# A four-layer transformer on one core: the first batch of relative attention sent through DRAM before the tables, and the experts' gate weights spread one group ahead with the last group closed in halves

## The chip, the cores and the metric

The kernel runs on one core of a Trainium2 chip. The core has five engines with an instruction queue each: TensorE (PE, matrix products into PSUM; its weight loads are shown as PEld), VectorE (DVE), ScalarE (ACT), GpSimd (POOL) and SyncE (SP, which here issues every DMA). The metric is the device time of one execution in microseconds, as the median of the runs. All data is float32.

## The reference, cut to what matters

Four layers, each followed by a residual sum and a layer norm over the last axis (128):

```
x = norm(x + relative_attention(x))     # 16 batches of 256 tokens, 16 heads of 8
x = norm(x + local_layers(x))           # 6 rounds of windowed attention and feed-forward
x = norm(x + causal_attention(x))       # 16 heads of 8
x = norm(x + experts(x))                # 8 experts, the best 2 by gate
```

The change touches the first and the last. Relative attention adds to the plain logits three terms that depend on the clipped distance of the two positions:

```
a_q, a_k, a_v = Eq[rel], Ek[rel], Ev[rel]          # rel: distance clipped to -64..64
logits = (q.k + q.a_k + k.a_q + a_q.a_k) * scale
out = softmax(logits) @ v  +  sum over m of softmax(logits)[l, m] * a_v[l, m]
```

The experts compute, for every token, all eight experts and keep two:

```
gates = softmax(x @ gate_w);  the two best: sel (0 or 1), tok_w = sum of the two gates
h = gelu(x @ w1[e] + b1[e]);  y[e] = h @ w2[e] + b2[e]
out = sum over e of y[e] * sel[e] * tok_w
```

## The kernel before, in words

**Relative attention** (`relative_attention`) works on one batch of 256 tokens at a time, in eight turns per batch (`NU = 8`, the table `TURNS`). `run(at)` emits the steps of turn `at % 8`; a step marked -1 works for the next batch, 0 for this one, 1 for the last. The turns from -8 to -1 hold batch 0's preparation alone. In order these are: `turn` (L317, the tokens transposed on PE), `project` (L326, q and k; L336 adds an end term on POOL), `rearranged` for k and then for q, `diagonal` (L405, a mask multiplied in on POOL), `rq_half` and `rq_corners` from k, `rk_half` and `rk_corners` from q (L419 and L444 on PE, with ACT copying the rq results out at L458 and L467 and DVE adding the position table `pp` or `ppc` at L478 and L488). Turn 0 begins with batch 0's second `rk_half` and ends in the first `weights` (L513 and L525 on PE, L535 on DVE), which the exponentials (L551) and everything else of the batch follow.

`rearranged` is a round trip through DRAM: POOL permutes (L385, one buffer `r_perm` for k and q), four DMAs write the rows to DRAM (L388, `r_rowsk` or `r_rowsq`), and four more read them back spread over the partitions (L393, `r_dk` or `r_dq`), each after its rows have landed.

Ahead of these turns stand the tables. Two of them (`toeplitz`, L793 on PE, `tq` and `tk`) are built from the small tables `Eq` and `Ek`, which are loaded turned, one element at a time (L770); their end values (`eqb`, `ekb`) go into L336 and L346. `prod` and `frow` (L818 to L822) make a row that is written to DRAM (L824) and read back in sliding windows (`windows`, L840: `r_winp`, `r_winpc`; `r_winv` and `r_winvc` come from a table of `Ev` rows that L827 to L829 put into DRAM). PE turns the windows over with the matrix `anti` (L878), and DVE copies the results to `pp`, `ppc`, `tv`, `tvc` (L882, L884). Memsets clear the term tiles `r_rq` on POOL and `r_rkc` on DVE.

The order of the instructions within each of PE, ACT, DVE and POOL is that of the program from `first` on, set by `env.in_order(first)`, where `first` stands behind the tables; for the tables themselves, and for SP, a scheduler chooses it.

**Experts** (`experts`) takes the 16 batches in eight groups of two (512 tokens, four tiles of 128). `turn(g)` transposes the tokens (L1780), `score(h)` makes the gate values of half of the groups (L1793 on PE, maximum and difference on DVE, exponential on ACT at L1805), and `choose(h)` finds the two best by counting on DVE (L1812 to L1829, one step of it, L1821, on POOL) and writes them spread into `e_wide`. For each group, `first` multiplies by w1 (L1840) with the gelu on ACT (L1847), `turn_gates` transposes the gates (L1854, copied out by ACT at L1856 as `e_wT`), `weigh` spreads them over the experts' rows on PE (L1865) and multiplies them into the gelus on DVE (L1867, `e_hT`), `second` multiplies by w2 (L1876) and adds b2 (L1883), sums with the tokens on DVE (L1886), and takes the statistics (L1894, L1895 on DVE; L1897 to L1901 on POOL). `finish` scales on ACT (L1907) and stores (L1915). `small()` gives one of four PSUM banks, `big()` one of two pairs of banks, which `weigh` takes both. The order of the loop is

```
for g in range(NG):
    turn_gates(g + 1); first(g + NH); second(g); weigh(g + 1); finish(g - 1)
finish(NG - 1)
```

with the four first groups' `first`, `turn_gates(0)`, `weigh(0)` and `choose(1)` ahead of it; it is kept on PE, ACT, DVE and POOL by `env.in_order(begin)`.

## Time and profile before

| | |
|---|---|
| runs shown, us | 4129.33, 4126.4, 4128.36; median 4128.36 |
| profiled execution, us | 4126.21 |
| its span, us | 4124.3 |
| mean granted clock of PE | 0.991 |
| PE busy | 4012.5 us, 97% |
| first weights matmul of relative attention | at 57.45 us |
| first transposes of the experts | at 3997.94 us |
| last matmul of the experts | ends at 4115.0 us |

The page gives busy time by engine and by slices of the span; the chain of waits follows back from the last instruction what released each step. A timeline line has the start, the duration, the engine, the line of the kernel, what is written from what, and in brackets how long the engine stood idle before it and what ended that. Durations of matmul groups count from the first start to the last end. The granted clock is 1.00 at full speed.

### The profile page before, as it was taken

The page shows a single profiled execution, that of the slowest core. Times are in us where ns is not written, and L with a number is a line of the kernel's source. Part 1 is how long each engine was busy: PE and PEld are TensorE (multiplying, and loading weights), DVE is VectorE, ACT ScalarE, POOL GpSimd, SP SyncE. Part 2 cuts the span into 40 slices and gives each one's busy share as a digit, 9 for nine tenths or more (in the row PEclk, how much of TensorE's full clock was granted, in tenths as well). Part 3 has the DMA queues.
Part 4 walks back from the last instruction along what each step waited for, and adds up shares of the span by engine and source line. Part 5 has one row for each costly group of instructions (what it writes and reads, how often), then busy time and mean ns, then how long its engine had stood idle before and what let it go on. Part 6 is the DMA issues. An engine that isn't in the chain of part 4 may idle for free.

```text
span 4124.3 us, 141653 instructions
## 1 busy us (share of the span) xinstructions
PE 4012.5 (97%) x57932; PEld 2937.4 (71%) x57932; DVE 3285.5 (80%) x6379; ACT 3305.0 (80%) x11434; POOL 2783.4 (67%) x3334
## 2 busy tenths in 40 slices
PE   7999999899999999999999999999999999999998
PEld 5888888567677677667767776776777767656665
DVE  4666666788888888888888888888888888779974
ACT  3777766688888888888888888888888888879973
POOL 3333332788888888888888888888888888722221
PEclk8999999999999999999999999999999999999999
DMA  2101012100000000000000000000000000000000
GB/s 62 40 29 38 31 36 64 26 16 19 21 24 19 15 20 20 25 21 20 20 25 16 19 19 20 25 21 14 21 15 24 15 16 14 9 3 2 2 8 21
DMA packets 181813, 90.03 MB, mean 22 GB/s; under 512 B 142493, under 2 KB 173220, under 8 KB 181164
## 3 DMA queue, kind: packets, MB, share of 16 engines
q1 hardware_dynamic: 181164, 80.97, 7.4%
q8 instruction: 457, 7.49, 0.8%
q14 instruction: 192, 1.57, 0.1%
HBM read 38.49 MB, written 6.31 MB: 11 GB/s over the span
## 4 chain that ended last, share of the span: by engine, by line
PE 86%; POOL 6%; ACT 3%; issue 2%; DVE 1%; DMA 1%; SPq 0%; POOLq 0%; DVEq 0%; ACTq 0%
PE small L1250 16%; PE big L1100 12%; PE small L1157 8%; PE big L1225 7%; PE big L1172 5%; PE small L1347 3%; PE small L1331 3%; PE small L1315 3%; PE small L570 3%; PE big L525 3%; POOL a_u L1139 3%; PE small L1592 3%; PE big L1548 3%; PE big L513 3%; PE small L1225 2%
## 5 line engine op out<-in xcount | busy, mean ns | idle before, releaser
L1193 ACT ACTIVATE a_pr<-a_pr,a_nb 128x64 f32<-128x64 f32 x3072 | 1024.0, 338 | 5.7 <-DVE a_nb L1186 5.7
L1121 POOL TENSOR_TENSOR a_u<-a_u,a_r 128x1024 f32<-128x1024 f32 x384 | 901.3, 2371 | 25.9 <-DVE a_r L1116 21.2
L1139 POOL TENSOR_TENSOR a_u<-a_u,a_y 128x1024 f32<-128x1024 f32 x384 | 722.9, 1904 | 15.0
L1250 PE MATMUL small<-a_vo,a_g 128*128 128x128 f32 x6144 | 718.1, 275 | 1.6 <-DVE c_st L1465 1.6
L1250 PEld LDWEIGHTS small<-a_vo,a_g 128*128 128x128 f32 x6144 | 701.6, 192 | 2.6 <-ACT a_g L1243 2.5
L1111 ACT ACTIVATE a_sq<-big 128x1024 f32<-128x1024 f32 x384 | 391.4, 1021 | 260.2 <-PE big L1100 259.5
L1193 ACT ACTIVATION_READ_ACCUMULATOR a_pr<-a_pr,a_nb 128x1 f32 x3072 | 587.9, 191 | 0.0
L1157 PEld LDWEIGHTS small<-ident,a_u 128*128 128x128 f32 x3072 | 349.7, 141 | 142.8 <-POOL a_u L1139 91.0
L1128 DVE TENSOR_REDUCE a_ss<-a_sq 128x16 f32<-128x1024 f32 x384 | 445.6, 1200 | 0.0
L1157 PE MATMUL small<-ident,a_u 128*128 128x128 f32 x3072 | 402.3, 274 | 25.3 <-POOL a_u L1139 23.4
L1100 PE MATMUL big<-w_k,a_xs 128*128 128x512 f32 x768 | 382.0, 620 | 5.1 <-DVE a_r L1116 2.1
L1205 POOL TENSOR_TENSOR a_pr<-a_pr,a_rd 128x1024 f32<-128x1024 f32 x192 | 366.1, 1907 | 13.0 <-DVE a_rd L1204 13.0
L1100 PE MATMUL big<-w_q,a_xs 128*128 128x512 f32 x768 | 361.4, 593 | 0.0
L1172 PEld LDWEIGHTS big<-a_kT,a_qT 64*32 64x32 f32 x24576 | 261.4, 105 | 124.7 <-issue 74.8
L1180 DVE TENSOR_TENSOR a_pr<-big,w_band 128x1024 f32<-128x1024 f32 x192 | 234.6, 1222 | 109.0 <-PE big L1172 109.0
L535 DVE CUSTOM_DVE_ANT_0 r_lg<-big,r_rq 128x256 f32<-128x256 f32 x512 | 186.7, 421 | 152.7 <-PE big L525 126.4
L1112 DVE TENSOR_TENSOR a_u<-big,a_tak 128x1024 f32<-128x1024 f32 x192 | 235.1, 1224 | 83.9 <-ACT a_sq L1111 83.9
L1172 PE MATMUL big<-a_kT,a_qT 64*32 64x64 f32 x24576 | 293.1, 225 | 6.4 <-POOL a_kT L1150 3.5
L1233 ACT COPY a_g<-big 128x1024 f32<-128x1024 f32 x192 | 193.7, 1009 | 107.3 <-PE small L1225 106.8
L1100 PEld LDWEIGHTS big<-w_q,a_xs 128*128 128x128 f32 x768 | 142.6, 190 | 162.6 <-issue 127.4
L551 ACT ACTIVATE r_lg<-r_lg,r_nb 128x256 f32<-128x256 f32 x512 | 254.4, 508 | 2.8 <-DVE r_nb L535 2.8
L1574 ACT ACTIVATE c_lg<-c_lg,c_nb 128x256 f32<-128x256 f32 x512 | 255.6, 513 | 0.1
(290 smaller groups left out, 9316.9 us busy)
## 6 DMA issues: line engine op xcount, KB each, us to landing
a_xm<-a_xt SPq DMA_DIRECT2D x96, 96.0 KB
r_dk<-r_rowsk SPq DMA_DIRECT2D x64, 128.0 KB
r_dq<-r_rowsq SPq DMA_DIRECT2D x64, 128.0 KB
f_xt<-xa SPq DMA_DIRECT2D x96, 64.0 KB
f_xt<-xa SPq DMA_DIRECT2D x96, 63.5 KB
a_xt<-xa SPq DMA_DIRECT2D x80, 64.0 KB
a_xt<-xa SPq DMA_DIRECT2D x80, 63.5 KB
w_k<-in_L_ffn_Wqkv_dram SPq DMA_DIRECT2D x6, 512.0 KB
```

The lines of the kernel that those rows point to most:

```text
L1100: T.matmul(ps[:, c * 512 : (c + 1) * 512], lhsT=xs_of[i, b][:, t, 0:P], rhs=weights[i]["qk"[j]][:, c * 512 : (c + 1) * 512], start=True, s ...
L1111: A.activation(sq, ps3, AF.Square)
L1121: G.tensor_add(u, u, r)
L1128: V.tensor_reduce(ss[:, j], st[m]["sq", j], AX.X, ALU.add)
L1139: G.tensor_mul(u, u, bcast(y[:, j].unsqueeze(2), (P, H, DH)))
L1157: T.transpose(ps[:, k, :], u[:, o : o + P], ident)
L1172: T.matmul(ps[q0 : q0 + WIN, e, c, :], lhsT=qT[DH * e : DH * (e + 1), c, q0 : q0 + WIN], rhs=kT[DH * e : DH * (e + 1), c, t * P + q0 : t * ...
L1193: A.activation(s_["pr"][:, h], s_["pr"][:, h], AF.Exp, bias=s_["nb"][:, h : h + 1], accum_out=s_["den"][:, h : h + 1],)
L1205: G.tensor_mul(s_["pr"], s_["pr"], bcast(rd.unsqueeze(2), (P, H, DH)))
L1225: T.matmul(ps[win], lhsT=x[r, t, :], rhs=pT[r, :, o, :], start=(o == 0), stop=(o == 1),)
L1250: T.matmul(ps[:, 0:D], lhsT=st[m]["g"][:, h, :], rhs=weights[i]["vo"][:, h // 2, h % 2, :], start=(h == 0), stop=(h == H - 1),)
L1574: A.activation(lg[:, j], lg[:, j], AF.Exp, bias=nb[:, j : j + 1], scale=-1.0, accum_out=st[b, lc]["den"][:, h : h + 1],)
```

## The change

In relative attention the setup is reordered, and it is now in the program's order on SP too. Loads: x of batch 0, Wq, Wk, then Eq and Ek, the mask, `sel`, the `Ev` rows in DRAM, `anti`. Then batch 0 is turned and projected at once, and k is permuted and sent to DRAM (`there`); `rearranged` is split into `there` and `back`, and the sum with `eqb` is split off `project` as `shift` for batch 0. `prod` and `frow` come before the toeplitz tables. SP's order then is: k's rows, `r_winv`, k back, q's rows, `fx`, `r_winvc`, q back, `fe`, `r_winp`, `r_winpc`, and only then `ee`, `evs`, Wv, x of batch 1, `pick` and the other x. The memsets move behind the projection, those of `r_rq` clear only the half that is not written later, and the turned tables `pp`, `ppc`, `tvc` stand behind batch 0's first `rq_corners`.

In the experts `choose(h)` follows `score(h)` at once, `first` runs two groups ahead of the loop and three inside it, `weigh(g + 1)` stands before `second(g)` and `turn_gates(g + 2)` behind it. The last group is summed, normalised (on DVE) and stored in two halves, the first as soon as its half of `second` is done (`close`). Copies of the transposed tokens go to DVE for groups 1 and 3 alone, and four buffers hold the gelus instead of five.

```diff
-    def in_order(first):
+    def in_order(first, engines=ENGINES):
...
+            st[b].update(q=q, k=k)
+            if b:
+                shift(b)
+
+        def shift(b):
+            q, qe = st[b]["q"], fea.tile([P, S], F32, name="r_qe")
             for t in range(NT):
                 L = slice(t * P, (t + 1) * P)
                 G.tensor_scalar(qe[:, L], q[:, L], eqb[:, t : t + 1], None, ALU.add)
...
         def rearranged(b, n):
+            there(b, n)
+            back(b, n)
...
+            turn(0)
+            project(0)
+            there(0, "k")
...
+            winv = windows("v", evx, HD, P * HD, whole)
+            back(0, "k")
+            there(0, "q")
+            nc.sync.dma_start(fx, frow)
+            winvc = windows("vc", evx, HD, MAXD * HD, corner)
+            back(0, "q")
...
+            winp = windows("p", fx, 1, P, whole)
+            winpc = windows("pc", fx, 1, MAXD, corner)
...
+            nc.sync.dma_start(w["v"], I["L0_attn_Wv"])
+            load_x(1)
+            nc.sync.dma_start(pick, I["pick"].rearrange("p (g m) -> p g m", g=4))
+            shift(0)
+            for k in range(2):
+                G.memset(rq3[k][:, :, 1], 0.0)
+            turned(tv.rearrange("p s d -> p (s d)"), winv, HD, P * HD, None)
+            for k in range(2):
+                V.memset(rkc3[k], 0.0)
+            for at in range(-NU, -NU + 6):
+                run(at)
+            turned(pp, winp, 1, P, None)
+            turned(ppc, winpc, 1, MAXD, fe)
+            turned(tvc.rearrange("p s d -> p (s d)"), winvc, HD, MAXD * HD, ee)
...
+            if at == -NU + 6:
+                G.memset(spread, 0.0)
+            if at == -1:
+                G.memset(rq3[2][:, :, 1], 0.0)
+                V.memset(rkc3[2], 0.0)
...
-        env.in_order(first)
+        env.in_order(first, (*ENGINES, mybir.EngineType.SP))
...
+                if g == NG - 1 and k % NT == NT - 1:
+                    close(g, k // NT)
...
+        def close(g, j):
+            y = two.tile([P, NT, D], F32, name="e_yh")
+            added(y, g, j)
+            mv, rs = moments(y)
+            for t in range(NT):
+                V.tensor_scalar(
+                    y[:, t], y[:, t], mv[:, t, 0:1], rs[:, t : t + 1], ALU.subtract, ALU.mult
+                )
+            store(g, j, y)
...
             score(h)
-        choose(0)
-        for g in range(NH):
-            first(g)
+            choose(h)
+        first(0)
+        first(1)
         turn_gates(0)
         weigh(0)
-        choose(1)
+        first(2)
+        turn_gates(1)
         for g in range(NG):
-            if g + 1 < NG:
-                turn_gates(g + 1)
-            if g + NH < NG:
-                first(g + NH)
-            second(g)
+            if g + 3 < NG:
+                first(g + 3)
             if g + 1 < NG:
                 weigh(g + 1)
+            second(g)
+            if g + 2 < NG:
+                turn_gates(g + 2)
             if g:
                 finish(g - 1)
-        finish(NG - 1)
```

## The prediction

> **What bounds the kernel.** I read the page first. TensorE (PE) is busy 97% of the span, so the middle has nothing that this change could give; its two ends do. The first and last tenths of PE's row are below 9, and PEclk is 8 at the start. So I read the chain, PE's timeline and the stretches of both ends.

> ```profile
> PE 4012.5 (97%) x57932; PEld 2937.4 (71%) x57932; DVE 3285.5 (80%) x6379; ACT 3305.0 (80%) x11434; POOL 2783.4 (67%) x3334
> PE   7999999899999999999999999999999999999998
> PEclk8999999999999999999999999999999999999999
> ```

> Head, from the chain of waits (start, us, what) and from PE's and SP's timeline:

> ```profile
> 8.49 7.08 PE small L793 x16
> 31.25 5.50 DMA r_rowsq<-r_perm
> 38.30 5.43 DMA r_dq<-r_rowsq
> 38.76 0.58 PE L419 MATMUL big<-r_dk,r_tq 32*128 32x128 f32 x2 [8.36 <-POOL r_dk L405]
> 47.74 0.58 PE L419 MATMUL big<-r_dq,r_tk 32*128 32x128 f32 x2 [3.94 <-POOL r_dq L405]
> 57.45 0.65 PE L513 MATMUL big<-ident,r_rk 128*128 128x128 f32 x4
> 59.87 2.50 SPq L388 DMA_DIRECT2D r_rowsk<-r_perm  x4
> 70.83 1.89 POOL L405 TENSOR_TENSOR r_dk<-r_dk,r_mask 128x1024 f32<-128x1024 f32 x1 [4.62 <-DMA r_dk<-r_rowsk]
> ```

> Batch 0 goes k to DRAM and back, then q to DRAM and back, and only then do the weights (L513, 57.45) begin. The trip begins late: the tables (L793) precede the projection on PE, and SP puts other loads between.

> Tail, PE's timeline, then stretches (PE, PEld, DVE, ACT, POOL busy, PEclk, DMA, GB/s):

> ```profile
> 4069.57 1.05 PE L1876 MATMUL small<-e_w,e_hT 128*128 128x128 f32 x8
> 4077.99 2.27 PE L1876 MATMUL small<-e_w,e_hT 128*128 128x128 f32 x8 [2.13 <-DVE e_hT L1867]
> 4088.06 2.35 PE L1876 MATMUL small<-e_w,e_hT 128*128 128x128 f32 x8 [2.04 <-DVE e_hT L1867]
> 4098.26 2.36 PE L1876 MATMUL small<-e_w,e_hT 128*128 128x128 f32 x8 [2.04 <-DVE e_hT L1867]
> 4108.48 2.36 PE L1876 MATMUL small<-e_w,e_hT 128*128 128x128 f32 x8 [2.62 <-DVE e_hT L1867]
> 4086.00:4088.00 2.00, 0.02 (x1) 0.00 (x0) 1.93 (x7) 0.59 (x1) 0.86 (x2) 1.00 0.00 0
> 4088.00:4090.00 2.00, 1.94 (x8) 1.74 (x9) 1.14 (x2) 0.96 (x3) 0.84 (x3) 0.52 0.00 0
> 4119.70 1.65 ACT L1907 ACTIVATE e_o<-e_y,e_nm,e_rs 128x128 f32<-128x128 f32 x4 [8.58 <-POOL e_nm L1901]
> ```

> In the last four groups PE waits for e_hT, and then runs eight matmuls in 2.3 us instead of 1.05, at a granted clock of 0.52.

> **Experts, part by part.** Warm prices on PE: first 3.44 (4056.58 to 4060.01), turn_gates 0.59, weigh 1.07, second 4.47; a round with a first is 9.56 (4055.01 to 4064.57).

> *Removed.* The four holes, 2.13 + 2.04 + 2.04 + 2.62 = 8.8, since weigh(g+1) now stands before second(g), and DVE's 2.33 of e_hT lies under 4.47 of second. The slow restarts with them: second(4) to second(7) take 6.3 to 6.5, so about 1.9 each, 7.5. The holes around second(1) (0.56, 0.77, 0.36, where choose(1) held DVE): 1.7. What is late next is ACT's e_wT, below.

> *Added, the start.* choose(0), 9.2 on DVE (4017.41 to 4026.64), now precedes score(1)'s maximum. It can start at 4010.85, when the first exponential is done, and ends near 4020.1; maximum and subtraction 0.6, exponential 0.3, table load 1.28: the first gelu at 4022.4, not 4019.15. PE has four small banks; it fills them by 4021.85 as before (the fourth is score(1)'s, released at 4020.7) and stands until 4023.1: 1.25. On ACT the other gelus follow PE's 0.86, so nothing more is lost. choose(1) runs 4021.1 to 4030.3, behind it e_hT(0) (weigh(0) ends 4029): ready long before second(0).

> *Added, three waits on e_wT.* PE's row before weigh(0) has 0.82; it stays. turn_gates(6) and (7) are each followed at once by their weigh, no first between: 0.82 twice, 1.6.

> *Forward from 4016.7:* first(0) to 4021.85; wait to 4023.1; first(1), turn_gates(0), wait, weigh(0) to 4029.0; first(2), turn_gates(1), first(3), weigh(1) 8.5 to 4037.5; second(0) and turn_gates(2) to 4042.6; four rounds of 9.57 to 4080.9; 0.82 + 1.07 + 4.47 + 0.59 = 6.95 to 4087.85; 6.36 to 4094.2; second(7) to 4098.7. Before, PE ended at 4115.0: gain 16.3. (The pieces above give 18.0 - 1.25 - 1.6 = 15.1; the rest is in 0.1 gaps. I take the forward sum.)

> *The halved end.* Before, 9.3 from PE's end to the span's. Now the first half's sum waits on DVE for y(6) (to 4096.7), costs 0.4 + 0.85, then POOL, queued behind nm(6) until 4098.8, 1.05 (power on 128x2, between 0.57 for x1 and 1.05 for x4, so 0.73), two scalings 0.65: DVE is free at 4100.55. The second half pays 0.4 + 0.85 + 1.2 + 0.65 to 4103.65, and the store 2.95 as before (4121.35 to 4124.3): 4106.6. The tail is 7.9; gain 1.4. The two added store issues lie on SP, idle there. **Experts: 17.7.**

> **Head, part by part.** SP's issues up to anti keep their prices (to 10.05 before; an element-wise table blocks the next issue 1.26). w["v"], pick, ee, evs and load_x(1) are moved behind the trips. The projection needs x, wq, wk, moved by 4 to 5 us by the 0-4 stretch (50 GB/s); transposes to k take 17.29 to 21.2 = 3.9, so r_perm is ready near 9 and SP near 10.15. SP is the later: rowsk at 10.15. From the first rowsk issue to POOL's r_dk, batch 1 took 59.87 to 70.83 = 11.0: 21.1, plus up to 1.3 for the 512 KB of r_winv now issued between (I take 0.4): 21.5. Here POOL must have done perm q (after rowsk landed, 15.6), eqb's sums 1.2 and two strided memsets. A memset of 2048 elements took 1.81; strided, between that and the 3.52 of 4096: I take 1.81, done 21.3; at 3.52, 24.7. So r_dk ends at 23.4, not at 38.7.

> rowsq starts on SP at 16.25, behind dk's four issues. Before, 31.25 to landing at 43.73 was 12.5: r_dq masked 28.75 to 30.7. On SP fx and winvc stand between, each waiting for a lane of dk; dq0 would wait for the last of these lanes anyway.

> PE: rq_half(0) and rq_corners(0), 3.3 (38.76 to 42.07), end at 26.8. Then PE's order holds the turned tables pp, ppc, tvc, whose loads SP issues after dq: fe twice, winp, then winpc behind dq0's landing, 27.3 to 27.9, landing 2.6 later (27.12 to 29.75 before): 30.0 to 30.5; tables to 31.3, rq_half(1) 2.1, rk_half(1) at 33.5 instead of 47.74: 14.2. This wait takes the place of the one for r_dq, which would allow 30.7. DVE's memset of rkc3[2], 1.76, now stands between rk_half(1) and rk_corners(1); DVE had 1.23 idle there: 0.6 lost, and project(1) behind the same psum release shifts as much. **Head: 13.6**; ends: 16.4 (PE waits only for r_dq) and 10.6 (winpc 3 us later, as for the rows that took 5.5 rather than 2.6).

> Covered: prod and both toeplitz on PE (9.5 to 18.6 by 1.86 + 7.08), tv, rkc memsets, both under the k trip, which would show only if it ended before 20.7. Batch 1 needs SP by 59.87 - 13.6 = 46.2; its 13 last x loads at 0.72 (11 took 7.95) from 33 end at 42.4, slack 3.8.

> **Sum.** 13.6 + 17.7 = 31.3. The profiled execution took 4126.2 (span 4124.3 and 1.9 outside): 4094.9, span 4093.0. It lies 2.15 below the median 4128.36; against the median 4097.

> **The clock, row and rule.** After holes of 2.04 the granted clock was 0.52; after 0.82 (4033) it stayed 1.00. The new hole of 1.25 lies between, nearer 0.82: nothing, at worst 1.9, and 3.8 more if the two holes of 0.82 slowed too. [...]

> **Rivals.**
> 1. *The row trips are held up in SP's lanes* (in the program each issue waits for the landing of the one eight before; winpc behind dq0, x loads behind ee). For it: the change adds such waits. Against: each landing is within 5.5. The head gives 8: 4128.4 - 25.7 = 4102.7. If SP were free only 13.6 after 46.2, batch 1's wait would eat the head whole: 4110.7.
> 2. *The start of the experts slows the clock:* gain 12.0 instead of 17.7: 4102.7.
> 3. *The clock stays up in the head,* PE's holes being shorter than the 8.4 before L419: rq_half and rk_half (2.1 at 0.50) take half, twice 1.05 and 1 in the corners: 4094.
> 4. *Slower: the experts run at the half clock throughout.* 4004 to 4012 shows 0.50 with PE 2.00 of 2.00 busy, so busy is not enough. The 76 us from 4022.4 would double: +76 - 31 = 4173. It decides once 31 us of this work run at 0.50. Against: the 512-wide matmuls stand at 1.00 from 4020 on.
> 5. *No effect,* a head and tail that hide each other: they lie at opposite ends of one PE-bound chain, so no.

> **Numbers.** Forecast 0.68, rivals 1 and 2 0.13 and 0.09, 3 0.06, 4 and anything else slower 0.03, no effect 0.01. The two worst ends together, 10.6 + 12.0, give 4106; with batch 1 held a little, 4109. The best, 16.4 + 19 and a little clock, 4091. Range 4090 to 4109. 0.2% (8.3 us, about what a measurement here can tell) is cleared by all but rival 4 and no effect: faster 0.96, same 0.01, slower 0.03.

> **What would show it.** Right: first rowsk near 10, r_dk near 21.5, a PE wait of about 3 for r_winp or r_winpc, the r_dq matmuls near 33.5, first weights near 44; no PE wait on e_hT, last matmuls 1.05, experts from 3984 to 4093. Wrong: rowsk much after 10, a DVE or POOL wait in front of r_dk, x loads ending after 46, PEclk 0.5 after the first gelu.

## The result, and the profile after

The changed kernel takes 4104.93 us (median; 4102.1 to 4106.04) against 4127.82 for the kernel before (4126.4 to 4129.33): a ratio of 0.9943 with a 95% interval of 0.9926 to 0.9961, so 22.9 us less. The forecast was 4097.0, 31.3 less. Its profiled execution took 4106.04, its span is 4103.3: 21.0 under the span of before.

The page, PE's row of busy times, its slices and the granted clock:

```profile
PE 4011.1 (98%) x57932; PEld 2934.4 (72%) x57932; DVE 3288.3 (80%) x6381; ACT 3300.4 (80%) x11432; POOL 2775.3 (68%) x3334
PE   8999999899999999999999999999999999989998
PEclk9999999999999999999999999999999999999999
```

The head, from the timelines of SP, POOL and PE (start, us, engine, line, what; in brackets the idle time before and what ended it):

```profile
10.27 2.55 SPq L395 DMA_DIRECT2D r_rowsk<-r_perm  x4
22.89 1.89 POOL L417 TENSOR_TENSOR r_dk<-r_dk,r_mask 128x1024 f32<-128x1024 f32 x1 [3.04 <-DMA r_winvc<-r_evx]
22.98 2.67 SPq L405 DMA_DIRECT2D r_dq<-r_rowsq  x4
26.88 0.59 SPq L850 DMA_DIRECT2D r_winp<-r_fx  x1
31.24 1.89 POOL L417 TENSOR_TENSOR r_dq<-r_dq,r_mask 128x1024 f32<-128x1024 f32 x1 [2.01 <-DMA r_dq<-r_rowsq]
31.75 0.77 PE L862 MATMUL small<-r_winp,r_anti 128*128 128x128 f32 x2 [3.69 <-DMA r_winp<-r_fx]
32.62 2.02 PE L862 MATMUL small<-r_winvc,r_anti 128*128 128x512 f32 x2
36.45 0.42 PE L431 MATMUL big<-r_dq,r_tk 32*128 32x128 f32 x2
43.89 1.13 PE L456 MATMUL big<-r_dq,r_tkc 32*64 32x64 f32 x32 [2.55 <-DVE r_rkc L500]
46.82 0.74 PE L525 MATMUL big<-ident,r_rk 128*128 128x128 f32 x4
```

The order is the one foretold: k's rows leave at 10.27, PE waits 3.7 for a table instead of for q, and the first weights start at 46.82 instead of 57.45. Two things stand differently: the tables and r_dq come later than forecast (r_winp by 1.3 to 1.8 us, the masked r_dq by 2.4), and PE waits 2.55 for DVE just before batch 1's projection (the steps of L326, behind the corners).

The experts, PE's timeline, every wait after the first `first`:

```profile
4018.97 3.70 PE L1864 MATMUL small<-e_xT,e_w 128*128 128x512 f32 x8 [0.60 <-ACT e_gl L1871]
4023.93 1.14 PE L1889 MATMUL big<-e_wT,e_esel 32*128 32x512 f32 x8 [0.82 <-ACT e_wT L1880]
4077.89 1.14 PE L1889 MATMUL big<-e_wT,e_esel 32*128 32x512 f32 x8 [0.73 <-ACT e_wT L1880]
4084.86 1.14 PE L1889 MATMUL big<-e_wT,e_esel 32*128 32x512 f32 x8 [0.73 <-ACT e_wT L1880]
4093.56 1.16 PE L1901 MATMUL small<-e_w,e_hT 128*128 128x128 f32 x8 [0.66 <-DVE e_yh L1927]
```

No wait for e_hT is left. From the experts' first transposes to the span's end it is 108.4 (3994.93 to 4103.30) instead of 126.3 (3997.94 to 4124.26).

So the head gives 10.6 at the first weights and the experts 17.9, and yet the spans differ by 21.0. Followed by the same instructions in both traces, the lead is 9.7 at the first exponential of batch 2, 9.0 at 690 us, 5.8 at 720, 4.9 at 850, 4.7 at 3590 and 3.0 when the experts begin. The middle, whose work the change leaves as it is (only SP's order in relative attention is pinned there), took 6.7 back. Most went at two places, 3.3 near 700 and 1.7 near 3600. The first of them, a hole in PE's work (a time in which it stands idle), by PE's timeline, before:

```profile
706.73 1.09 PE L570 MATMUL small<-ident,r_lg 128*128 128x128 f32 x8 [2.06 <-DVE r_y L641]
```

and by stretches of 3.41 us, before (the stretch, its length, then PE, PEld, DVE, ACT and POOL busy, PEclk, DMA, GB/s):

```profile
702.07:705.48 3.41, 2.60 (x23) 1.98 (x20) 0.00 (x0) 3.04 (x10) 0.00 (x0) 1.00 0.31 96
705.48:708.90 3.42, 2.17 (x18) 2.01 (x20) 2.71 (x15) 0.59 (x1) 0.86 (x2) 1.00 0.53 141
708.90:712.31 3.41, 3.41 (x30) 2.86 (x30) 2.94 (x14) 1.93 (x6) 0.80 (x2) 1.00 0.23 48
```

The same place in the changed kernel, PE's timeline:

```profile
697.70 1.09 PE L582 MATMUL small<-ident,r_lg 128*128 128x128 f32 x8 [2.10 <-DVE r_y L653]
```

and its stretches:

```profile
695.62:699.04 3.42, 1.34 (x12) 1.34 (x13) 1.92 (x11) 1.16 (x4) 0.85 (x2) 1.00 0.68 194
699.04:702.45 3.41, 3.41 (x16) 2.25 (x15) 1.48 (x8) 0.00 (x0) 0.81 (x3) 0.50 0.17 35
702.45:705.86 3.41, 3.41 (x18) 3.41 (x17) 2.47 (x13) 2.36 (x7) 0.00 (x0) 0.50 0.14 32
```

It is the same wait, 2.06 and 2.10 long. Before, it is followed by the full clock; after, by 6.8 us at half of it (a granted clock of 0.50, called the half clock below). The stretches are not chosen freely: in both traces the recorded changes of the granted clock (27 before, 19 after) lie at whole multiples of 3.413 us from one another, to 0.007 us, and these are the windows of that grid. Before, the hole lies across a boundary and each window keeps 2.2 us or more of work; after, it lies whole in one window and leaves 1.34, 0.39 of it. That gave the theory that the runs were to test: **a window of this grid in which PE was busy less than some four tenths halves the clock of the next, the grid does not start with the kernel, and so the middle gains or loses some us from one execution to the next.** The rival: the loss is built into the changed program.

Over the whole middle the changed kernel stood at the half clock for 27.3 us, with PE busy for 25.3 of them; the kernel before for 17.1 and 16.0. If half of that work's time is what the half clock adds (second's eight matmuls took 2.3 instead of 1.05), it makes 4.7 of the 6.7, an estimate; the other 2.0 are not accounted for.

### The profile page after: what moved, and what is told of

Read it like the earlier page. It is cut to its first block, busy times and chain, and to the rows that moved or that the text cites. A ratio compares the mean times of both kernels' runs of the same rounds, so it can differ in the third digit from the quotient of the medians.

```text
span 4103.3 us, 141645 instructions
## 1 busy us (share of the span) xinstructions
PE 4011.1 (98%) x57932; PEld 2934.4 (72%) x57932; DVE 3288.3 (80%) x6381; ACT 3300.4 (80%) x11432; POOL 2775.3 (68%) x3334
## 4 chain that ended last, share of the span: by engine, by line
PE 87%; POOL 6%; ACT 3%; issue 2%; DVE 1%; DMA 1%; SPq 1%; POOLq 0%; DVEq 0%; ACTq 0%
PE small L1274 16%; PE big L1124 12%; PE small L1181 8%; PE big L1249 7%; PE big L1196 5%; PE small L1371 3%; PE small L1355 3%; PE small L582 3%; PE big L537 3%; PE small L1339 3%; PE small L1616 3%; PE big L1572 3%; POOL a_u L1163 3%; PE big L525 3%; PE small L1249 2%
## 5 line engine op out<-in xcount | busy, mean ns | idle before, releaser
L1145 POOL TENSOR_TENSOR a_u<-a_u,a_r 128x1024 f32<-128x1024 f32 x384 | 900.5, 2368 | 28.1 <-DVE a_r L1140 23.1
L1181 PE MATMUL small<-ident,a_u 128*128 128x128 f32 x3072 | 402.6, 274 | 25.4 <-POOL a_u L1163 22.9
L1124 PEld LDWEIGHTS big<-w_q,a_xs 128*128 128x128 f32 x768 | 142.3, 190 | 162.3 <-issue 126.3
```

Of the source, the lines that this page charges most:

```text
L1124: T.matmul(ps[:, c * 512 : (c + 1) * 512], lhsT=xs_of[i, b][:, t, 0:P], rhs=weights[i]["qk"[j]][:, c * 512 : (c + 1) * 512], start=True, s ...
L1145: G.tensor_add(u, u, r)
L1181: T.transpose(ps[:, k, :], u[:, o : o + P], ident)
```

## The experiments

All of it in one table; the experiments follow in the order in which they ran. "Batch 2" is the first exponential of batch 2 in relative attention (number 64, counted from 0), "middle" the time from there to the experts' first transposes, "experts" from there to the end of the span. These come from the one profiled execution of each kernel, the last two columns from its timed runs against the kernel before on the same chip (whose medians were 4127.2 to 4128.7).

| kernel | first weights | batch 2 | middle | experts | span | median | ratio, 95% |
|---|---|---|---|---|---|---|---|
| before | 57.45 | 101.29 | 3896.7 | 126.3 | 4124.3 | 4127.82 | |
| after | 46.82 | 91.56 | 3903.4 | 108.4 | 4103.3 | 4104.93 | 0.9926 to 0.9961 |
| head_only | 45.56 | 89.19 | 3896.9 | 129.7 | 4115.7 | 4121.06 | 0.9973 to 0.9992 |
| experts_only | 57.59 | 101.28 | 3901.1 | 112.7 | 4115.1 | 4112.71 | 0.9949 to 0.9972 |
| same_again | 46.37 | 91.17 | 3897.6 | 109.1 | 4097.9 | 4102.43 | 0.9925 to 0.9954 |
| memset_early | 44.15 | 88.59 | 3898.6 | 109.1 | 4096.2 | 4096.38 | 0.9907 to 0.9940 |
| tables_first | 46.79 | 88.41 | 3900.2 | 109.9 | 4098.5 | 4102.94 | 0.9923 to 0.9952 |
| rotary_pool | 46.24 | 91.21 | 3894.3 | 108.6 | 4094.1 | 4098.21 | 0.9914 to 0.9947 |
| experts_reordered | 45.81 | 90.38 | 3904.4 | 101.9 | 4096.7 | 4096.59 | 0.9904 to 0.9933 |
| all_together | 46.51 | 87.27 | 3895.7 | 105.1 | 4088.0 | 4089.33 | 0.9889 to 0.9918 |
| hole_doubled | 45.77 | 89.86 | 3901.0 | 109.8 | 4100.7 | 4104.79 | 0.9922 to 0.9956 |
| together_old_tables | 43.73 | 84.71 | 3901.0 | 101.3 | 4087.0 | 4087.92 | 0.9880 to 0.9913 |

### One half of the change at a time, and the same again

**head_only** has the changed `relative_attention` and the experts of before; **experts_only** the reverse; **same_again** is the changed kernel, unaltered.

> The changed relative attention with the experts of before. Theory (grid): the start is 10.6 us earlier at the first weights and 9.6 after batch 1's wait, as in the changed kernel; between there and the experts the gain is changed only where a hole of PE of some 2 us falls whole into one 3.41 us window of the clock or is split between two, and that differs from execution to execution: ahead by 3 to 10 us when the experts begin, time 4127.8 less 3 to 10, so 4118 to 4125, and the spots that lose are not all those of the changed kernel's profile (699 and 3597 us). Rival (built in): the changed program loses the 6.6 us each time, at the same two spots: 3.0 ahead at the experts' start, 4124.8. The experts then take 126.4 us to the end of the span, as before, with four waits on e_hT.

> The relative attention of before with the changed experts. Theory: the experts take 108.4 us from their first transposes to the span's end instead of 126.4, so 18.0 less: 4109.8, with 2 to 3 us either way from holes in the middle. Rival: part of the 18.0 came from the head (the phase in which the experts met the clock's windows); then the experts take 110 us or more here, with a granted clock of 0.5 somewhere after 4022, and the time is 4112 or more.

> The changed kernel once more, nothing altered: a second profile. Theory (grid): the start repeats to some 0.3 us (first weights near 46.8), the waits of PE in the middle repeat in length, but which of them are followed by a half clock differs; with the share of a window in which PE was busy at 0.42 or less the next window is at 0.50, above it is not. Time between 4100 and 4108. Rival (built in): again a half clock from 699 to 706 and from 3597 to 3600, 6.6 us lost between 70 and 3650 against the kernel before.

Measured: head_only was 12.1 ahead at batch 2 and still 11.9 ahead when the experts began; it lost nothing in the middle. experts_only, whose program is that of before up to the experts, fell 4.4 behind it in the middle. same_again was 10.1 ahead at batch 2 and 9.2 at the experts, where the first profile of the same program had 3.0 left; it had no half clock at 695 to 706, but one at 3607. The built-in rival falls: the same program loses 6.7 in one execution and 0.9 in the next, and an untouched middle loses 4.4.

The experts' time moves too. Those of before took 126.3 and 129.7, the changed ones 108.4 to 112.7. For experts_only the rival's numbers came (112.7, and 4112.71): its clock stood at 0.50 from 4006 to 4030, through the gate's matmuls and both first `first` steps (10.1 us of PE for the two, 9.1 in the changed kernel's profile). So the experts' gain is 17 to 18 in most pairs of profiles, and 3 to 4 of what one profile shows there are the windows' too. With half of PE's busy time at the half clock taken off (an estimate; that time is 27.1 and 33.3 us in the two profiles of the old experts, 13.4 to 23.1 in the seven of the changed ones) the experts take 112.8 and 113.0 in the old order and 100.6 to 101.9 in the changed one: 11 to 12 of the gain are the order's own, the rest is half clock that the changed experts met less of.

### memset_early

```diff
-            for k in range(2):
+            for k in range(3):
                 V.memset(rkc3[k], 0.0)
...
                 G.memset(rq3[2][:, :, 1], 0.0)
-                V.memset(rkc3[2], 0.0)
```

> The changed kernel with the memset of the third rkc tile put beside the other two, where DVE waits 6 us for the tables. Theory: DVE's add of rkc then runs from 40.4 to 41.7 instead of 42.4 to 43.8, PE's wait of 2.55 before the corners falls to 0.5, no window is idle enough to halve the clock there, and the corners, the projection and the first weights run at the full clock: first weights 2.1 (the memset alone) to 3.5 us (with the clock) before 46.8; the time 2 to 3.5 lower than the changed kernel's, 4101.4 to 4103. Rival: batch 1's trip through DRAM sets the path again and takes the gain back: r_dk of batch 1 still masked at 60.3, time as the changed kernel's.

Measured, PE's and DVE's timeline of memset_early:

```profile
40.41 1.38 DVE L500 TENSOR_TENSOR r_rkc<-big,r_ppc 64x512 f32<-64x512 f32 x2
41.93 0.69 PE L456 MATMUL big<-r_dq,r_tkc 32*64 32x64 f32 x32 [0.46 <-DVE r_rkc L500]
44.15 0.66 PE L525 MATMUL big<-ident,r_rk 128*128 128x128 f32 x4 [0.47 <-DVE r_rk L490]
```

The wait of 2.55 became 0.46, the corners ran in 0.69 instead of 1.13, and the first weights came 2.2 to 2.7 earlier than in the two profiles of the changed kernel; at batch 2 it was 2.6 to 3.0, so the rival (batch 1's trip takes it back) falls. The median, 4096.38, is 6.1 to 8.6 lower than the changed kernel's two and below the 4101.4 to 4103 expected. The head explains 2.6 to 3.0 of that; the spread of the middle is large enough for the rest, but where the rest came from was not shown.

### tables_first

```diff
-            winvc = windows("vc", evx, HD, MAXD * HD, corner)
-            back(0, "q")
             for k in range(2):
                 ...
             winp = windows("p", fx, 1, P, whole)
             winpc = windows("pc", fx, 1, MAXD, corner)
+            back(0, "q")
+            winvc = windows("vc", evx, HD, MAXD * HD, corner)
...
             turned(ppc, winpc, 1, MAXD, fe)
+            run(-NU + 6)
             turned(tvc.rearrange("p s d -> p (s d)"), winvc, HD, MAXD * HD, ee)
```

> The changed kernel with the loads of r_winp and r_winpc (and fe) issued ahead of q's way back, r_winvc behind it, and the large turned table vc put behind rk_half(1) on PE. Theory: PE's wait of 3.7 for r_winp comes from SP's order alone; the small tables are ready when the corners end (28), rq_half(1) follows at once, and the wait is then for r_dq, whose way back starts 1 to 2 us later than 22.98: rk_half(1) at 34 to 35 instead of 36.4, first weights 1.5 to 2.5 earlier than 46.4 to 46.8. Rival: q's way back pays for all of it (each load put ahead of it delays r_dq by as much): rk_half(1) at 36 or later, no gain.

Measured, SP's and PE's timeline of tables_first:

```profile
25.64 2.67 SPq L405 DMA_DIRECT2D r_dq<-r_rowsq  x4
35.70 0.58 PE L431 MATMUL big<-r_dq,r_tk 32*128 32x128 f32 x2 [5.24 <-POOL r_dq L417]
```

The rival holds for the first weights: q's way back started 2.66 later on SP, the wait for r_winp became one of 5.24 for r_dq, and the weights began at 46.79. (The r_dq matmuls began at 35.70, between the theory's 34 to 35 and the rival's 36.) Tables and q's rows share one queue, and in these two orders whichever stands first there delays the other (here q's way back by 2.66; in the changed kernel r_winp, used 4.9 after its issue, in the kernel before 3.2). The clock is not separated from this: it became full at 39.4 here and at 36.85 in the changed kernel's first profile, which may have taken back the 0.75 that the r_dq matmuls were earlier. The lead of 2.8 that it has at batch 2 came later: PE's wait for batch 1's r_dk was 1.9, and no half clock followed it.

### rotary_pool

DVE stands 6.7 us near 690 for the load of the local layers' rotary table, because the scaling of that table has its place in DVE's order there; the transposition that PE's hole of 2.1 waits for is behind it. DVE's timeline of the changed kernel:

```profile
697.12 0.29 DVE L954 TENSOR_SCALAR w_rot<-w_rot 128x256 f32<-128x256 f32 x1 [6.67 <-DMA w_rot<-in_rot_dram]
```

```diff
-            V.tensor_scalar_mul(rot[:, 0:2], rot[:, 0:2], QK_SCALE)
+            G.tensor_scalar_mul(rot[:, 0:2], rot[:, 0:2], QK_SCALE)
```

> The changed kernel with the scaling of the rotary table, for whose load DVE stood 6.7 us at 690, put on POOL. Theory (grid): the hole of 2.1 in PE at 696 goes, and with it the chance of a half clock behind it, which cost 3.3 in the changed kernel's profile: no window at 695 to 706 with PE busy 0.42 or less; the last exponential of relative attention 2.0 earlier against the same start in every execution, against the first profile 5 earlier. Rival: PE's wait is only handed on, since POOL or DVE's next reader waits for the same load: less than 1 us, and still a hole of 1 to 2 there.

Measured: PE has no hole there, and from exponential 300 to the last of relative attention it takes 468.1. With the hole (2.06 to 3.16 long in eight profiles) it was 470.1 to 470.8 where the clock stayed full (five) and 473.1 to 473.7 where it did not (three: after, tables_first, experts_reordered). The wait itself costs 2.0 to 2.7, and the half clock behind it some 3 more (473.5 and 473.7 against 470.1 to 470.5 for holes of 2.06 to 2.10). The wait is in the kernel before as well; whether a half clock followed differed from profile to profile, even of one program (after, same_again).

### experts_reordered

```diff
-        for h in range(2):
-            for g in range(NH * h, NH * (h + 1)):
-                turn(g)
-            score(h)
-            choose(h)
+        for g in range(NG):
+            turn(g)
+        score(0)
+        rank(0)
+        score(1)
+        pick_two(0)
         first(0)
         first(1)
         turn_gates(0)
+        rank(1)
         weigh(0)
+        pick_two(1)
...
+            if g + 2 < NG:
+                turn_gates(g + 2)
             second(g)
-            if g + 2 < NG:
-                turn_gates(g + 2)
```

`rank` and `pick_two` are `choose` cut in two behind the comparisons; e_wT has three buffers, and the last group's second half a PSUM bank of its own.

> The changed kernel with the experts' start and end in another order: all eight turns first, score(1) between the two halves of choose(0), choose(1) in halves around the first e_hT, turn_gates(g+2) ahead of second(g), the last group's two halves in two banks. Theory: the experts' 108.4 to 109.1 from first transposes to end hold a wait for e_gw of 2.4, gelus that wait for score(1)'s exponential behind choose(0) (6 us), two waits of 0.73 for e_wT and one of 0.66 for the bank. First gelu 17 after the first transposes instead of 23.3 (21 in the second profile), none of the three late waits; 100 to 102.5, 6 to 8 less. Rival: DVE's choosing (2 x 9.2) sets the pace of the start whatever the order, so weigh and second wait on DVE instead: 2 to 4 less.

Measured: 101.9, 6.5 to 8 less than most profiles of the changed experts. The first gelu stands 15.8 behind the first transposes instead of 23.3, the wait of 0.60 behind the first gelus and the three of 0.66 to 0.73 near the end are gone, and no wait on DVE came in their place, as the rival had it. But the size is in part the clock's: PE worked 6.8 us at the half clock in these experts, 13.4 to 23.1 in the seven profiles of the changed ones. With half of that taken off (an estimate as above) they take 98.5 against 100.6 to 101.9, PE's idle time up to its last matmul falls from 5.3 to 6.5 (after, same_again, rotary_pool) to 2.1, and the end behind that matmul grows from some 7 to 8.8. So some 2 to 3.5 are the order's own, the size that the rival had given; the same experts took 105.1 in all_together (13.7 at the half clock) and 101.3 in together_old_tables (6.8). Whether the new order itself makes the half clock shorter was not settled. The middle of this execution was the longest of all (3904.4), so its span shows little of it.

### all_together

memset_early, tables_first, rotary_pool, experts_reordered, and q's shift put behind the permutation of k on POOL:

```diff
             st[b].update(q=q, k=k)
-            if b:
-                shift(b)
...
             there(b, n)
+            if n == "k":
+                shift(b)
             back(b, n)
```

> The changed kernel with the early memset, the tables first, q's shift of batch 1 and later behind the permutation of k on POOL, the rotary scaling on POOL, and the reordered experts. Theory: the pieces add, since they lie at different places of one PE-bound chain: 2.5 + 2 + 1 + 2 to 5 + 6 to 8 = 13.5 to 18.5 less than the changed kernel's 4102.4 to 4104.9: 4085 to 4091. Rival: at the start they share one path, batch 1's trip through DRAM, which takes 2 to 3 back: 4088 to 4094.

Measured: 4089.33 (4087.46 to 4089.82), in both ranges. First weights at 46.51, although memset_early alone had 44.15; tables_first alone had 46.79, and together_old_tables below leaves it out.

### hole_doubled

```diff
+            V.tensor_reduce(spare, bcast(rot[:, 0, 0, 0:8].unsqueeze(2), (P, 8, 256)), AX.X, ALU.max)
             V.tensor_scalar_mul(rot[:, 0:2], rot[:, 0:2], QK_SCALE)
```

> The changed kernel with a reduction of some 2.2 us that does nothing for the result put on DVE behind the landing of the rotary table, in front of the transposition that PE waits for: the hole of 2.1 at the end of relative attention becomes 4.1. Theory (grid): a hole of 2.1 halves the clock only where some 2 us of it fall into one window, in 3 of the 8 profiles so far that have it; one of 4.1 leaves 2 us or more idle in some window wherever it falls, so a half clock follows in each execution: from the middle of relative attention to its last exponential 475.5 to 475.8, against 470.1 to 470.8 (hole of 2.1, clock full), 473.1 to 473.7 (hole of 2.1, half clock behind it) and 468.1 (no hole); the time 3.5 above the changed kernel's on average. Rival: the half clock is not decided by the idle share of a window; then the added 2.0 are all, 472.3 to 472.8.

Measured, PE's timeline:

```profile
697.64 1.06 PE L582 MATMUL small<-ident,r_lg 128*128 128x128 f32 x8 [1.26 <-DVE r_rd L655]
```

Neither came: the hole did not grow to 4.1, it shrank to 1.26, because PE's order changed with the edit and took one more step of weights (L582, L525 and L537 once more) ahead of the wait. The stretch took 470.3, with the full clock. It decides nothing between the two; the series below does it where the order is pinned.

### together_old_tables

all_together without tables_first.

> The four pieces together without the tables first: early memset, q's shift behind the permutation, rotary scaling on POOL, reordered experts. Theory: tables_first moved the wait and gained nothing at the first weights, so leaving it out costs nothing there: first weights at 44 instead of 46.5, r_dk of batch 1 masked near 55.7, which leaves PE a hole under 1 us before it; the start 13 to 14.5 ahead of the kernel before (64th exponential near 87), the time 4086 to 4090, equal or lower than with them (4089.3). Rival: the gain of 2.8 that tables_first had behind batch 1's wait was its own; then the 64th exponential is at 88 or later here, the time 4090 to 4092.

Measured: 4087.92 (4081.83 to 4089.80), 0.9897 of the kernel before (0.9880 to 0.9913), the lowest of all, 14.5 to 17.0 under the changed kernel's two medians; against all_together its interval overlaps. First weights at 43.73 and batch 2 at 84.71, 16.6 ahead of before and so more than either side expected: r_dk of batch 1 comes early enough that no window there falls under 0.79, so no half clock either. The rival falls. Against all_together the first weights are 2.8 earlier; the clock became full at 36.7 here and at 41.1 there, and the two runs do not tell how much of the 2.8 is the order on SP and how much the clock.

### hole_series, twice

```diff
+            if at % 8 == 2 and 18 <= at < 122:
+                n = 512 + 96 * (at // 8 - 2)
+                V.tensor_reduce(idle, bcast(mask4.unsqueeze(2), (P, 4, n)), AX.X, ALU.max)
             run(at)
```

> The changed kernel with 13 reductions that do nothing for the result, of 2.3 to 8 us, on DVE, one per batch of relative attention from batch 2 on, each longer than the last: DVE's slack takes up a part of each and the rest is a hole in PE, from nothing to some 5 us, in an order of work that is pinned. Theory (grid): a window of 3.41 us in which PE was busy 0.41 or less is followed by a half clock, one with 0.49 or more is not; so no hole under 1.9 us halves the clock, every hole of 4.1 or more does, and those of 2.0 to 4 do or do not by where they fall, not in the order of their length. Rival (length alone): there is one length, between 1.9 and 2.6, below which none and above which every hole is followed by a half clock.

> The same kernel as hole_series, looked at once more. Theory (grid): the same 13 holes with the same lengths to some 0.3 us, but for those between 2.0 and 4 us the half clock comes behind others than in the first look, again as the busy share of the windows says (0.41 or less, 0.49 or more). Rival (length alone): the same holes are followed by a half clock in both.

Measured: the first five reductions (2.3 to 3.9 us) leave PE no hole, DVE's slack takes them up; the other eight make holes of 0.52 to 3.32, the same in both executions to 0.02 (none reached 4.1, so what the theory says of longer ones was not tried); the kernel took 4125.54 and 4125.10, one execution each. For each hole, PE's busy share in the windows it lies in, and the clock of the next:

| hole | hole_series | clock | hole_series_again | clock |
|---|---|---|---|---|
| 0.52 to 1.72 (four) | 0.50 or more | 1.00 | 0.50 or more | 1.00 |
| 2.12 | 0.38 | 0.50 | 0.38 | 0.50 |
| 2.52 | 0.73, 0.54 | 1.00 | 0.56, 0.71 | 1.00 |
| 2.92 | 0.79, 0.36 | 0.50 | 0.62, 0.53 | 1.00 |
| 3.32 | 0.45, 0.58 | 1.00 | 0.80, 0.23 | 0.50 |

The hole of 3.32 by stretches, columns as above, in hole_series:

```profile
667.27:670.69 3.42, 1.53 (x56) 1.26 (x48) 3.38 (x17) 2.23 (x9) 0.55 (x2) 1.00 0.02 5
670.69:674.10 3.41, 1.98 (x18) 2.01 (x19) 1.73 (x7) 0.38 (x1) 2.81 (x6) 1.00 0.10 23
674.10:677.51 3.41, 3.41 (x55) 3.07 (x53) 1.48 (x8) 3.25 (x12) 2.71 (x5) 1.00 0.25 69
```

and in hole_series_again:

```profile
661.65:665.06 3.41, 2.73 (x96) 2.37 (x90) 3.41 (x11) 1.53 (x7) 0.00 (x0) 1.00 0.08 31
665.06:668.47 3.41, 0.77 (x7) 0.80 (x8) 2.46 (x12) 0.69 (x4) 2.74 (x7) 1.00 0.04 8
668.47:671.89 3.42, 3.42 (x19) 3.42 (x18) 0.74 (x3) 1.70 (x5) 1.07 (x3) 0.50 0.22 35
```

Length alone falls: a hole of 3.32 leaves the clock full in one execution and halves it in the next, a hole of 2.12 halves it in both while 2.52 does in neither. The share of the window fits all sixteen holes: 0.38 or less was followed by the half clock, 0.50 or more by the full one. The one window between the bounds of 0.41 and 0.49 that the theory had set (0.45, the hole of 3.32 in hole_series) was followed by the full clock; the bounds do not say which.

## Why the prediction was right, and where its terms were not

The sign, the two places and the range were right (4104.93 within 4090 to 4109). Of the 31.3, 21.0 came in the profiled pair: head 9.7 for 13.6, experts 17.9 for 17.7, and 6.7 lost where nothing was forecast. That the time still fell inside the range is luck in part: the range's upper end stood for a slower head and a slower start of the experts, and no term of it for the middle.

**Experts, 17.7: mechanism right, and the size by parts that made up for each other.** The four holes are gone and `second` runs at the full clock; from first(0) to PE's end it takes 83.1 (82.0 forecast, 98.3 before), a gain of 15.2 for 16.3. "Added, the start" was 0.60 instead of 1.25, the three waits on e_wT were 0.82 and twice 0.73. Missing was a wait of 0.66: the last group's second half writes the bank that the halved end is still reading. The tail is 7.2, forecast 7.9, before 9.2. Another 0.7 came ahead of first(0) (18.1 from the first transposes, before 18.8), where the forecast had nothing.

**Head, 13.6: mechanism right, size wrong.** The step that failed first is "tables to 31.3, rq_half(1) 2.1, rk_half(1) at 33.5": it began at 36.45, 2.95 late. 1.3 to 1.8 of this is the landing of the small tables (31.75 instead of 30.0 to 30.5). SP issued r_winp at 26.88 and r_winpc at 27.51, in time by the forecast (27.3 to 27.9 for r_winpc), but behind q's four loads on the same queue: PE started on r_winp 4.9 after its issue, in the kernel before 3.2 (26.02 to 29.20), where the forecast took 2.6 for r_winpc. q's rows themselves took 6.6 and 6.0 there and back instead of the 5.5 and 5.4 of before. The other order on SP, tables_first, moved the wait to r_dq instead of removing it. The rest is the price of the three tables on PE: they took 2.83 (31.75 to 34.58), and the forecast left 0.8 to 1.3 for them. vc's two matmuls took 2.02 at the half clock and 1.02 at the full clock before, so 1.0 of it is the clock; but the 0.46, 0.66 and 1.02 that the three took before are more than the forecast left as well. The second step is "DVE's memset of rkc3[2] ... 0.6 lost": it held up the add that frees the bank, PE waited 2.55, and memset_early puts its price at 2.2 to 3.0. It did not show in the sum to the first weights (10.4 from rk_half(1), as forecast), most likely because the clock became full at 36.85 and gave about as much back: the mean clock over this stretch was 0.85, before 0.53. Another 0.9 went at batch 1's trip, 0.8 of it behind PE's wait for r_dk (3.10 long, before 2.61), which two windows of half clock followed, before one.

**"The middle has nothing that this change could give": the step that cost most.** It can give nothing, but it isn't a constant. Eight profiles with the same middle have 3896.7 to 3904.4 for it. With half of PE's busy time at the half clock taken off (15.9 to 35.1 us; an estimate) they have 3886.5 to 3890.7, so the clock makes the larger part of the spread, not all of it. The kernel before was profiled with the shortest of them, the changed one with the second longest, and head_only, same_again and experts_only show that the loss is not built into the change. The same forecast against an average middle (3899.9) on both sides would have been short by the head's 3.9 alone.

**The clock.** The forecast asked how long a hole must be (0.52 after holes of 2.04, 1.00 after 0.82). The traces show that the length alone does not say it: the clock changes on a grid of 3.413 us, whose phase against the kernel's start lies anywhere from 0.1 to 2.9 us in the fourteen profiles (2.34 before, 2.72 after), and in a window of it 2.1 us idle of 3.42 were enough (busy 1.34, near 700), where as long a hole across a boundary was not (busy 2.60 and 2.17, before). Of the changed experts' waits of 0.60 to 0.82 (five, behind the first `first`) none was followed by the half clock while PE had work. The experts' term of 7.5 for the slow restarts rested on where the windows lay as well, though in both profiles of the old experts all four holes (2.0 to 2.6) were followed by the half clock; rounds of 10.1 to 10.2 us (second at 4077.99, 4088.06, 4098.26 and 4108.48 before) are close to three windows of the grid, 10.24, so that the next hole falls where the last one fell.

**Rivals.** 1 (trips held up in SP's lanes, the head gives 8, 4102.7) is nearest in size, but its mechanism came in part only: SP issued the tables in time, and it was the loads themselves, one behind the other, that took longer; and most of what brought the time to 4104.93 was lost in the middle, of which it says nothing. 3 (the clock stays up in the head) did not happen: the 9s of PEclk at the start of the profile's page only mean that no change was recorded yet (the trace's first record of the clock is at 36.85). The starts of neighbouring pairs of 32-row matmuls tell it, 0.21 us apart up to 36.8 and 0.11 after. 2 and 4 in their form did not come, but the half clock at the experts' start is real in both kernels and cost experts_only 3 to 4. 5 is excluded by head_only and experts_only.

**Open.** By its terms the change should give about 27 (9.7 to 10.1 at batch 2 and 17 to 18) wherever the middle is the same on both sides; the medians gave 22.9 and 24.7, and the halves alone 6.1 (3.3 to 11.1 by its interval) and 14.5 (11.6 to 21.0). The whole's intervals allow 27 (head_only's own profile, with 12.1 at batch 2, lies above its interval), and a spread of some 10 us between single executions of one kernel can hide the difference, but whether 3 us are lost in some other place was not settled.

## What to carry to other kernels

Search for PE's holes of 2 us and more at every change of stage, not only near the edit: the one near 700 cost 2.0 to 2.7 us itself, in three of eight profiles with some 3 us more from the half clock behind it, and shifting the work moves all of them on the clock's grid of 3.413 us. So compare a change by the stretches that it touches, in two or more profiles, and take the rest as scatter. A load's consumer that stands in an engine's order ahead of older work (the rotary scaling on DVE) or a memset in front of an add that frees a bank cost PE 2 to 3 us here, and moving it to an idle engine or an idle moment took a line or two each.
